# Leaky ReLU and residual sum of layer 1's input, moved from VectorE and GpSimd to ScalarE and TensorE, in a four-layer fused kernel

## The chip, the core and the metric

The kernel runs on one core of one Trainium2 chip. The core has four compute engines that run side by side, each with its own queue: TensorE (PE, matrix products), VectorE (DVE), ScalarE (ACT) and GpSimd (POOL). A fifth, SyncE (SP), only starts DMA transfers here. The metric is the device time of one launch, in microseconds; lower is better.

## The reference

The input is x, 16 images of 192 channels and 32 x 32 pixels (1024 pixels), in float32. Four layers follow, each of the form x = x + f(norm(x)). Layer 0 is an mLSTM block, then a 3x3 convolution, a batch norm over all images and a leaky ReLU. Layer 1 is channel attention, layer 2 a state-space block with a selective scan in four directions, layer 3 a convolution over weighted shifts. What the change touches is the end of layer 0 and the beginning of layer 1:

```python
# end of layer 0: y is the convolution's output
y = (y - mu) / jnp.sqrt(var + 1e-05) * bn_g[None, :, None, None] + bn_b[None, :, None, None]
return jnp.where(y >= 0, y, 0.01 * y)
...
x = x + _L0_conv_ref(_gn(x), ...)
x = x + _L1_conv_ref(_gn(x), ...)
```

So per image: scale and shift each channel, take the larger of y and 0.01 y, add x, and go on to layer 1's group norm.

## The kernel before, in words

**Two parts.** `layer0` runs layer 0 for all images, up to the convolution's output before its batch norm, which goes to DRAM (`ydram`). The batch norm needs statistics over all images, so only then can `LayersB` begin, which does the rest. `setup` (L992) makes the batch norm's scale `bsc` and shift `bsh`, one column per group of 96 channels.

**The row of scans.** In `LayersB`, layer 2's selective scan is the backbone. It is cut into units: 128 lanes (32 channels x 4 states) by 1024 pixels, 192 units per image, 3072 in all. A unit needs: on ACT a decay (`decay`, L1987), on POOL an input (`inputs`, L1994), on DVE the scan itself (`scan`, L2002) and the product with C (`outputs`, L2011), on PE the sum over states (`sums`, L2044). In every eighth unit (`pooled`, L789: unit number 3 modulo 8) POOL makes the product instead (`weigh`, L2007). The tiles of this row turn over: two `h` in PSUM, three `xs` and three `hc` in SBUF, two each of `dl` and `du`, which are reloaded from DRAM for every four units (`fetch`, L1966).

**The pieces between.** All other work runs in the gaps of that row, as three streams of pieces: `front` makes the next units' inputs (`ahead`, L1876), `before` is `complete` (L1460: layer 2's end and layer 3 of the image before), `after` is `prepare` (L1236: the end of layer 0, layer 1 and the start of layer 2 of the image after). Each `yield` names the engine of the next piece. The order is written out while the program is built: `scans` (L1737) goes unit by unit, emits the unit's own instructions, and lets a stream go on where `fits` (L1824) says that by the planner's own clocks there is room. Those clocks add fixed prices per instruction (`Metered.RATES`, L797) and do not see the chip. Where PE would be left without work, `warm` (L2049) puts in matmuls of zeros.

**DMAs.** All loads and stores of this part are started by SP, in the order in which the program emits them. `post` (L913) notes a transfer; `flush` (L932) or `need` (L922) sends it when the planner's clock says that its source is ready, or that it is needed. An image's end matters here: `prepare` of the image after next begins near unit 184 and runs over into the next image, while `complete` of the image just scanned begins with the load of that image's scan output (`yh<-yd`, posted at L1480) and of x (`cx<-x1d`), a matmul with `on384` for the mean (L1488) and a subtraction on DVE (L1491).

**The stage that changes** (`prepare`, L1252 to L1268), per image:

- ACT scales and shifts both channel groups of `y` in place (two passes of 96 x 1024);
- for each of four halves ACT writes 0.01 y into a PSUM bank, and DVE takes the maximum of y and that bank into y;
- for each channel group POOL adds y to x (96 x 1024);
- x is stored for later (`x0d`), and `norm6` (L1132) takes its statistics on ACT.

`y` lives in the slot `pb`, which has room for three groups, `x` in the slot `pa`. `whole` and `view` give both as slices of fixed tiles. Most helpers record their instructions through `Metered`, so that these carry the line L817 in the profile; groups are told apart by the tiles' names.

Of the kernel before, what the change touches and what calls it, by code (L numbers as in the profile page):

```python
# [11 lines left out]
F32 = mybir.dt.float32  # L12
BF16 = mybir.dt.bfloat16
AF = mybir.ActivationFunctionType
ALU = mybir.AluOpType
# [5 lines left out]
L = H * W  # L21
HL = L // 2
P6 = 96
# [8 lines left out]
def half(hf):  # L32
    return slice(hf * HL, (hf + 1) * HL)


def matmuls(nc, out, pairs):
    n = len(pairs)
    for i, (l, r) in enumerate(pairs):
        nc.tensor.matmul(out, lhsT=l, rhs=r, start=(i == 0), stop=(i == n - 1))
# [821 lines left out]
class LayersB:  # L861
# [130 lines left out]
    def setup(self):  # L992

        tc, nc, cx, wp, I, NB = self.tc, self.nc, self.cx, self.wp, self.I, self.NB
        dp = self.dp
        self.dqd = dp.tile([6, 128, 9, 128], F32, name="dqd")
        self.dvd = dp.tile([2, 2, 128, 9, P6], F32, name="dvd")
        self.vd = dp.tile([P6, 2, L], F32, name="vd")
        self.x0d = dp.tile([P6, 2, L], F32, name="x0d")
        self.x2d = dp.tile([P6, 2, L], F32, name="x2d")  # L1000
        self.xdr = dp.tile([K, 2 * N, L], F32, name="xdr")
        self.dld = dp.tile([K, 3, 128, L], F32, name="dld")
        self.dud = dp.tile([K, 3, 128, L], F32, name="dud")
        self.yd = dp.tile([3, 128, L], F32, name="yd")
        self.zd = dp.tile([NB, 3, 128, L], F32, name="zd")
        self.x1d = dp.tile([NB, P6, 2, L], F32, name="x1d")


        bn_g, bn_b = self.vec("bn_g", P6), self.vec("bn_b", P6)
        self.bsc = wp.tile([P6, 2], F32, name="bsc")  # L1010
        self.bsh = wp.tile([P6, 2], F32, name="bsh")
        with tc.tile_pool(name="b_pre0", bufs=1) as pre:
            st = pre.tile([P6, 2, NB, 12], F32, name="st")
            for a in range(2):
                nc.scalar.dma_start(
                    st[:, a], self.sdram[:, a * P6 : (a + 1) * P6, :].rearrange("b p s -> p b s")
                )
            mv = pre.tile([P6, 2, 2], F32, name="mv")
            for a in range(2):
                nc.vector.bn_aggr(mv[:, a, :], st[:, a].rearrange("p b s -> p (b s)"))  # L1020
            sd = pre.tile([P6, 2], F32, name="sd")
            nc.scalar.activation(sd, mv[:, :, 1], AF.Sqrt, bias=cx.eps5[0:P6])
            nc.vector.reciprocal(sd, sd)
            nc.vector.tensor_mul(self.bsc, sd, bn_g)
            nc.vector.tensor_mul(sd, mv[:, :, 0], self.bsc)
            nc.vector.tensor_sub(self.bsh, bn_b, sd)


        self.blk6 = wp.tile([P6, P6], F32, name="blk6")
        nc.vector.tensor_scalar(self.blk6, cx.blk6, 1.0 / L, None, op0=ALU.mult)  # L1030
        self.offb = wp.tile([P6, P6], F32, name="offb")
        nc.sync.dma_start(self.offb, I["c_off48"])
        self.temp = wp.tile([P6, 2], F32, name="temp")
        for a in range(2):
            for j in range(2):
                nc.sync.dma_start(
                    self.temp[48 * j : 48 * j + 48, a : a + 1],
                    I["temperature"][2 * a + j : 2 * a + j + 1].unsqueeze(0).to_broadcast([48, 1]),
                )

        self.dw2b = self.vec("dw_b", 128)
        self.pads = [wp.tile([128, H + 2, W + 2], F32, name="pad%d" % i) for i in range(2)]
        for t in self.pads:
            nc.gpsimd.memset(t, 0.0)

        self.xx = wp.tile([128, 3, L], F32, name="xx")
        self.fixed, self.turned, self.views, self.whole = {}, {}, {}, {}
        for tag, n, bufs in (("pa", 2, 1), ("pb", 3, 1), ("p4", 1, 2), ("c4", 1, 3), ("cx", 2, 1)):
            self.fixed[tag] = [wp.tile([128, n * L], F32, name=tag + str(i)) for i in range(bufs)]
            for i, t in enumerate(self.fixed[tag]):  # L1050
                (nc.gpsimd if i % 2 else nc.vector).memset(t, 0.0)
        c4 = self.fixed["c4"]
        self.fixed["o4"] = c4[0:2]
        self.fixed["d3"] = [c4[2][:, 256 * i : 256 * i + 256] for i in range(4)]
        self.fins = []
        self.ms = [wp.tile([128, 2, C], F32, name="m%d" % i) for i in range(2)]
        for t in self.ms:
            nc.gpsimd.memset(t, 0.0)
# [177 lines left out]
    def prepare(self, b):  # L1236

        nc, cx, sm, I = self.be, self.cx, self.sm, self.I
        one = lambda i: bass.ds(i, 1)
        ch = lambda a: slice(a * P6, (a + 1) * P6)  # L1240
        yield "SP", 0
        y = self.slot("pb", [P6, 2, L], "y0")
        self.post(y, y, self.ydram[one(b)].rearrange("o (a p) l -> p (o a) l", p=P6))
        x = self.slot("pa", [P6, 2, L], "x0")
        self.post(x, x, I["x"][one(b)].rearrange("o (a p) l -> p (o a) l", p=P6))
        wv = self.weight(I["w_vT"].rearrange("(a p) o -> p a o", p=128), [128, 2, C])
# [3 lines left out]
        wq_ = [w_qk(0)]  # L1250
        yield "SP", 2
        for a in range(2):  # L1252
            yield "ACT", 0, y
            self.need(y)
            nc.scalar.activation(
                y[:, a, :], y[:, a, :], AF.Identity, scale=self.bsc[:, a : a + 1], bias=self.bsh[:, a : a + 1]
            )
        for a in range(2):
            for hf in range(2):
                yield "ACT", 0  # L1260
                p = self.mm()[0:P6, :]
                nc.scalar.activation(p, y[:, a, half(hf)], AF.Copy, scale=0.01)
                yield "DVE", 0
                nc.vector.tensor_max(y[:, a, half(hf)], y[:, a, half(hf)], p)
            yield "POOL", 0, x
            self.need(x)
            nc.gpsimd.tensor_add(x[:, a, :], x[:, a, :], y[:, a, :])
        self.post(x, self.x0d, x)  # L1268
        yield from self.norm6(x)

# [2 lines left out]
        for a in range(2):  # L1273
# [4 lines left out]
            v = self.p4([P6, L], "v")  # L1278
# [4 lines left out]
        for m in range(3):  # L1283
# [11 lines left out]
            for t0 in (0, 4):  # L1295
                yield "PE", 0
                p = self.mm()
# [85 lines left out]
        for m_, w_ in ((m1, w1), (m2, wpf)):  # L1383
            yield "PE", 0, w_
            self.need(w_)
            p = self.mm()[0:P6, 0 : 2 * C]
# [5 lines left out]
        for hf in range(2):  # L1392
            for a in range(2):
                yield "PE", 0, vs[hf]
                self.need(vs[hf])
                p = self.mm()[0:P6, :]
# [4 lines left out]
        x = self.slot("pa", [P6, 2, L], "x1")  # L1401
# [6 lines left out]
        for a in range(2):  # L1408
            for hf in range(2):
                yield "PE", 0, x  # L1410
                self.need(x)
                p = self.mm()[0:P6, :]
# [30 lines left out]
        for gs in ((0, 1), (2,)):  # L1443
            zs = [self.p4([128, L], "z") for g in gs]
            for g, z in zip(gs, zs):
                for hf in range(2):
                    yield "PE", 0, wz
                    self.need(wz)
                    p = self.mm()
# [723 lines left out]
```

## Time and profile before

| | |
|---|---|
| median of 3 runs | 14432.32 us (14414.68 to 14432.79) |
| the profiled execution | 14423.57 us |
| its span, first to last instruction | 14421.8 us |
| mean granted TensorE clock | 0.924 |
| the row of scans | about 3320 to 14280 us |
| one image in it | 681 to 683 us |
| HBM traffic | 1338 MB read, 341 MB written |

A group line of the profile reads: line, engine, operation, output <- inputs by tile name (numbers left out), shapes, count | busy time in all, mean of one in ns | idle time of the engine just before them, and what ended it. A wait line reads: engine, the line that waited <- what it waited for: total us, times, longest. A line in order of time reads: start and duration in us, engine, line, what it does, and in brackets how long the engine had been idle and what released it. PE shows each float32 matmul as two rows. SP's instructions are the starts of transfers, whose data move after them.

### The profile page before, as it was taken

To read this page: it belongs to the slowest core of one execution; us is meant where nothing else is said; L and a number is where in the kernel's file an instruction comes from. 1 tells how busy PE (TensorE), PEld (TensorE's weight loads), DVE (VectorE), ACT (ScalarE), POOL (GpSimd) and SP (SyncE) were. 2 spreads that over 40 slices of the span, in tenths; PEclk is the share of its full clock that TensorE was granted. 3 is DMA by queue.
4 is the path that set the end of the run, shared out by engine and by line. 5 is a ranking of instruction groups with operands and counts; after the bars stand their busy time and mean duration, and the time that the engine had idled before them with its cause. 6 is when DMAs were issued, how large, how long until landed. Compare 5 with 4: busy or idle time off the path is not lost. (4 is left out here: it accounts for less than half of the span.)

```text
span 14421.8 us, 185702 instructions
## 1 busy us (share of the span) xinstructions
PE 12156.5 (84%) x68912; PEld 4993.1 (35%) x68912; DVE 11832.7 (82%) x9085; ACT 8688.4 (60%) x12229; POOL 10928.7 (76%) x6319
## 2 busy tenths in 40 slices
PE   8999999987888888888888888788888888888877
PEld 4444444442233333333333333333333333333323
DVE  4444444447899999999999999999999999999996
ACT  3333333336667676767676666676676767676655
POOL 2222222216799999999999999999999999999995
PEclk9999999998999999999999999998999999999888
DMA  1000000014344444444444445444444444444432
GB/s 29 15 16 16 15 16 16 16 40 131 128 157 143 157 154 159 153 143 158 143 158 141 160 145 164 142 159 137 162 134 164 147 157 162 145 152 150 144 122 90
DMA packets 702528, 1707.95 MB, mean 118 GB/s; under 512 B 125456, under 2 KB 260065, under 8 KB 693985
## 3 DMA queue, kind: packets, MB, share of 16 engines
q1 hardware_dynamic: 688928, 1693.28, 36.0%
q8 instruction: 556, 9.11, 0.3%
q10 hardware_dynamic: 12736, 3.04, 0.1%
q14 instruction: 308, 2.52, 0.1%
HBM read 1338.12 MB, written 341.15 MB: 116 GB/s over the span
## 5 line engine op out<-in xcount | busy, mean ns | idle before, releaser
L1994 POOL TENSOR_TENSOR xs<-du,bb 128x1024 f32<-128x1024 f32 x3072 | 7196.6, 2364 | 424.9 <-DVE h L2002 418.5
L2002 DVE TENSOR_TENSOR_SCAN h<-h,xs 128x1024 f32<-128x1024 f32 x2688 | 6150.8, 2288 | 385.5 <-ACT h L1987 296.1
L1987 ACT ACTIVATE h<-dl,A 128x1024 f32<-128x1024 f32 x3072 | 3413.9, 1113 | 2420.4 <-DVE hc L2011 2268.5
L2011 DVE TENSOR_TENSOR hc<-h,cb 128x1024 f32<-128x1024 f32 x2688 | 3290.6, 1224 | 264.9 <-DVE h L2002 4.6
L817 PE MATMUL mm<-pad,dg 128*128 128x512 f32 (+1 forms) x5580 | 2667.4, 616 | 120.3 <-DMA dg<-dvd 39.9
L2044 PE MATMUL acc<-hc,sel 128*32 128x256 f32 x24576 | 2016.5, 415 | 800.5 <-DVE hc L2011 600.5
L629 POOL TENSOR_TENSOR D<-D,mask 128x256 f32<-128x256 f32 x768 | 543.6, 741 | 2101.7 <-DVE D L626 2101.7
L2044 PEld LDWEIGHTS acc<-hc,sel 128*32 128x32 f32 x24576 | 549.6, 112 | 2745.4 <-DVE hc L2011 1397.2
L817 PEld LDWEIGHTS mm<-pad,dg 128*128 128x128 f32 (+1 forms) x5580 | 958.7, 182 | 1494.0 <-issue 1285.7
L2007 POOL TENSOR_TENSOR hc<-hc,cb 128x1024 f32<-128x1024 f32 x384 | 905.7, 2359 | 205.1 <-DVE hc L2002 201.9
L817 PE MATMUL mm<-pa,wgt 128*128 128x512 f32 (+1 forms) x1408 | 781.6, 681 | 208.0 <-ACT pb L817 119.6
L2052 PE MATMUL acc<-ones,zero 128*128 128x512 f32 x1648 | 901.6, 678 | 0.0
L2002 DVE TENSOR_TENSOR_SCAN hc<-h,xs 128x1024 f32<-128x1024 f32 x384 | 875.6, 2280 | 16.7 <-ACT h L1987 12.5
L817 POOL TENSOR_TENSOR dlh<-dlh,e 128x512 f32<-128x512 f32 x384 | 489.4, 1275 | 233.5 <-ACT e L817 230.9
L817 POOL TENSOR_TENSOR c<-cx 96x768 f32<-96x768 f32 (+4 forms) x510 | 650.2, 1298 | 2.5 <-PE mm L817 2.5
L817 PE MATMUL mm<-c,xT 128*96 128x256 f32 x2048 | 575.9, 423 | 69.0 <-ACT c L817 68.2
L2031 PE MATMUL acc<-y,ident 128*128 128x512 f32 x576 | 354.2, 700 | 250.1 <-ACT y L2063 248.8
L817 POOL TENSOR_TENSOR duh<-dlh,xx 128x512 f32<-128x512 f32 x384 | 538.1, 1401 | 30.1
L393 PE MATMUL pc<-ypad,w_c 128*64 128x512 f32 (+1 forms) x1152 | 480.3, 664 | 74.3 <-PEq L753 41.5
L2063 ACT COPY y<-acc 128x512 f32<-128x512 f32 x384 | 411.4, 1071 | 150.7 <-PE acc L2044 149.9
L626 DVE SCALAR_TENSOR_TENSOR D<-D,s 128x256 f32<-128x256 f32 x768 | 271.7, 416 | 255.6 <-ACT D L622 255.6
L2052 PEld LDWEIGHTS acc<-ones,zero 128*128 128x128 f32 x1648 | 329.4, 215 | 431.8 <-issue 429.5
(334 smaller groups left out, 15907.5 us busy)
## 6 DMA issues: line engine op xcount, KB each, us to landing
dl<-dld SPq DMA_DIRECT2D x768, 512.0 KB
du<-dud SPq DMA_DIRECT2D x768, 512.0 KB
bb<-xdr SPq DMA_DIRECT2D x256, 512.0 KB
cb<-xdr SPq DMA_DIRECT2D x256, 512.0 KB
dld<-dlh SPq DMA_DIRECT2D x384, 256.0 KB
dud<-duh SPq DMA_DIRECT2D x384, 256.0 KB
dg<-dqd SPq DMA_DIRECT2D x270, 192.0 KB
dg<-dvd SPq DMA_DIRECT2D x180, 144.0 KB
```

What stands on the lines that cost most here:

```text
L393: nc.tensor.matmul(p[r, :], lhsT=w_, rhs=v, start=(n == 0), stop=(n == 14))
L629: nc.gpsimd.tensor_mul(d, d, mask)
L817: return f(out, *args, **kw)
L1987: self.nc.scalar.activation(self.h[u % 2], self.dl[n % 2], AF.Exp, scale=self.A[:, blk, n : n + 1])
L1994: self.nc.gpsimd.tensor_mul(self.xs[u % 3], self.du[n % 2], self.bb[blk])
L2002: self.nc.vector.tensor_tensor_scan(o, h, x, 0.0, op0=ALU.mult, op1=ALU.add)
L2007: self.nc.gpsimd.tensor_mul(h, h, self.cb[u % BLOCKS])
L2011: self.nc.vector.tensor_mul(self.hc[u % 3], self.h[u % 2], self.cb[u % BLOCKS])
L2031: nc.tensor.matmul(acc, lhsT=self.cx.ident, rhs=self.y[:, g, half(pair)], start=True, stop=False)
L2044: nc.tensor.matmul(self.acc[rows4(q), q4(s)], lhsT=self.sel, rhs=part(q), start=False, stop=(s + blk == BLOCKS),)
L2052: self.nc.tensor.matmul(self.acc, lhsT=cx.zero.to_broadcast([128, 128]), rhs=cx.ones.unsqueeze(1).to_broadcast([128, 4, 128]), start=False ...
L2063: self.nc.scalar.copy(y.rearrange("p (s w h) -> p s h w" if k % 2 == 0 else "p (s h w) -> p s w h", s=2, **turn), self.acc.rearrange("p (s ...
```

## The change

The leaky ReLU is written as 0.99 relu(y) + 0.01 y. `setup` makes four small columns `leak`: scale and shift times 0.99 and times 0.01. Per channel group ACT now makes 0.01 y into a third group of `y`'s slot (Identity) and 0.99 relu(y) in place (Relu). For each half PE adds three products with the identity matrix in one PSUM bank (relu part, 0.01 part, x), and ACT copies the bank into x. DVE's maxima, ACT's copies into PSUM and POOL's additions are gone. The third group of the slot serves both channel groups, one after the other. The number of pieces in the stage stays at twelve.

```diff
+        self.leak = wp.tile([P6, 4, 2], F32, name="leak")
+        for i, share in enumerate((0.99, 0.01, 0.99, 0.01)):
+            nc.vector.tensor_scalar(self.leak[:, i, :], self.bsh if i // 2 else self.bsc, share, None, op0=ALU.mult)
...
-        y = self.slot("pb", [P6, 2, L], "y0")
-        self.post(y, y, self.ydram[one(b)].rearrange("o (a p) l -> p (o a) l", p=P6))
+        y = self.slot("pb", [P6, 3, L], "y0")
+        self.post(y, y[:, 0:2, :], self.ydram[one(b)].rearrange("o (a p) l -> p (o a) l", p=P6))
...
         for a in range(2):
-            yield "ACT", 0, y
-            self.need(y)
-            nc.scalar.activation(
-                y[:, a, :], y[:, a, :], AF.Identity, scale=self.bsc[:, a : a + 1], bias=self.bsh[:, a : a + 1]
-            )
-        for a in range(2):
+            for i, f in ((1, AF.Identity), (0, AF.Relu)):
+                yield "ACT", 0, y
+                self.need(y)
+                nc.scalar.activation(
+                    y[:, 2 * i + a * (1 - i), :], y[:, a, :], f,
+                    scale=self.leak[:, i, a : a + 1], bias=self.leak[:, 2 + i, a : a + 1],
+                )
             for hf in range(2):
+                yield "PE", 0, x
+                self.need(x)
+                p = self.mm()[0:P6, :]
+                matmuls(nc, p, [(cx.ident[0:P6, 0:P6], v[:, half(hf)]) for v in (y[:, a, :], y[:, 2, :], x[:, a, :])])
                 yield "ACT", 0
-                p = self.mm()[0:P6, :]
-                nc.scalar.activation(p, y[:, a, half(hf)], AF.Copy, scale=0.01)
-                yield "DVE", 0
-                nc.vector.tensor_max(y[:, a, half(hf)], y[:, a, half(hf)], p)
-            yield "POOL", 0, x
-            self.need(x)
-            nc.gpsimd.tensor_add(x[:, a, :], x[:, a, :], y[:, a, :])
+                nc.scalar.copy(x[:, a, half(hf)], p)
         self.post(x, self.x0d, x)
```

## The prediction

> **What bounds the kernel now.** I read the busy times first, then the groups by line, then the waits of VectorE (DVE) and of the DMA queue (SP), and last the order of time around one image's end. I call the i-th scan of an image "unit i" (0 to 191); 16 images make 3072 units. From the page:
>
> ```profile
> PE 12156.5 (84%) x68912; PEld 4993.1 (35%) x68912; DVE 11832.7 (82%) x9085; ACT 8688.4 (60%) x12229; POOL 10928.7 (76%) x6319
> L1994 POOL TENSOR_TENSOR xs<-du,bb 128x1024 f32<-128x1024 f32 x3072 | 7196.6, 2364 | 424.9 <-DVE h L2002 418.5
> L2002 DVE TENSOR_TENSOR_SCAN h<-h,xs 128x1024 f32<-128x1024 f32 x2688 | 6150.8, 2288 | 385.5 <-ACT h L1987 296.1
> L2011 DVE TENSOR_TENSOR hc<-h,cb 128x1024 f32<-128x1024 f32 x2688 | 3290.6, 1224 | 264.9 <-DVE h L2002 4.6
> ```
>
> From about 3320 to 14280 us the kernel is one long row of scans, in which DVE is 93 to 94% busy and POOL 92 to 95% (windows of 1000 us). A unit takes 3.53 us from scan to scan; every eighth, whose product POOL makes, 2.2 us. Images repeat every 681 to 683 us, so whatever delays a scan counts, times some 15 images. The longest single waits of that row are not ACT's. Next, lines from the waits of DVE and of SP:
>
> ```profile
> DVE h L2002 <- ACT h L1987: 296.1, 275, 12.3
> DVE yh L817 <- PE mm L817: 65.2, 15, 8.2
> SPq L1962 <- POOL xs L1994: 5653.1, 685, 15.9
> ```
>
> The second line is 4.3 us each: DVE stands before the first `yh` subtraction of `complete`, because the matmul before it waits for `yh`'s load. The third says that SP, one queue in order, spends 39% of the span holding a reload of `du` or `dl` until POOL has read the old one; all that stands behind it waits too.
>
> **The removed and added work.** Groups by line, and by tile name:
>
> ```profile
> L817 DVE TENSOR_TENSOR pb<-pb,mm 96x512 f32<-96x512 f32 x64 | 42.8, 672 | 4.7 <-ACT mm L817 4.6
> L817 ACT ACTIVATE mm<-pb 96x512 f32<-96x512 f32 x64 | 37.4, 586 | 24.2 <-DVE pb L817 24.2
> L817 POOL TENSOR_TENSOR pa<-pa,pb 96x1024 f32<-96x1024 f32 x32 | 75.4, 2357 | 22.4 <-DVE pb L817 22.4
> L817 ACT ACTIVATE pb<-pb,bsh,bsc 96x1024 f32<-96x1024 f32 x32 | 38.0, 1232 | 26.6 <-DMA pb<-ydram 20.8 <-DVE row L1104 5.8
> L817 ACT COPY pa<-mm 96x512 f32<-96x512 f32 x64 | 37.0, 578 | 17.9 <-PE mm L817 17.9
> L817 PE MATMUL mm<-pa,ident 128*96 128x512 f32 x128 | 69.0, 622 | 0.0
> ```
>
> DVE loses 64 maxima of 0.67 us. In the order of time one does not cost that much: with it a unit is 3.92 us long (scan starts 7450.03 and 7453.95), 0.39 over 3.53; behind a product, before a pooled scan, 1.74 between starts against 1.14 elsewhere, 0.60. Per image 3 x 0.39 + 0.60 = 1.77, and 15 images: **27 us saved**. Image 0 runs before the scans, where its DVE, POOL and ACT pieces overlap; I take 0, bounds -4 and +4.
>
> POOL loses 32 x 2.36 = 75 us. POOL waits for DVE 418 us and DVE for POOL's `xs` only 80 us in all, near units that hardly touch this stage; I take 0, bounds -10 and 0.
>
> ACT loses 64 x 0.586, gains 64 x 0.578 and 32 more full passes of 1.23: +39 us in 14400, with ACT 60% busy. It costs where a decay (L1987) comes late: summed unit by unit, ACT work beyond a unit's length is 52 us per image before and 53 after (row durations, order of both built programs), so 0, bounds -2 and +2 an image, -30 and +30. PE gains 192 f32 matmuls of 69.0/64 = 1.08 us, 207 us, less 9 fewer warming matmuls of 901.6/824 = 1.09, in 2265 us of idle: 0 of its own. Four tiny DVE scalings in setup: 4 x 0.1.
>
> Both kinds of ACT copy stand above: into PSUM 586 ns, out of PSUM 578 ns; so the new copies cost what the old did. The Trainium skill, "ScalarE: Activation LUTs", Step-by-step, says that ScalarE writes faster to PSUM than to SBUF, which speaks against turning these copies round; these rows do not show it. By the rule the 64 copies would cost more than before, by an amount that the page does not price; by the rows, 0.5 us less in all.
>
> **What the change moves.** The stage now goes ACT, PE, ACT one half after the other, with one third slot of `y` for both channel groups, and the planner, which fits pieces into units, ends it 5 units later: the last copy stands at unit 5 of the next image instead of the last addition near unit 0. Two things follow in the built order of images 3 to 14. The store `x0d<-pa` waits for that copy, and on SP it now comes after unit 5's `du` reload; behind it come `out_x`, the `out_proj` weights, and `yh<-yd`. Before, `yh` stood ahead of that reload. And the first `yh` subtraction stands in unit 7 instead of 6. Before, from the order of time around one image's end:
>
> ```profile
> 8152.16 2.28 DVE L2002 TENSOR_TENSOR_SCAN hc<-h,xs 128x1024 f32<-128x1024 f32 x1
> 8155.59 0.80 SPq L929 DMA_DIRECT2D yh<-yd  x1
> 8159.20 6.96 POOL L1994 TENSOR_TENSOR xs<-du,bb 128x1024 f32<-128x1024 f32 x3
> 8163.89 0.52 SPq L1962 DMA_DIRECT2D du<-dud  x1
> 8164.56 5.32 PE L817 MATMUL mm<-yh,on 128*128 128x512 f32 x6 [4.19 <-DMA yh<-yd]
> 8169.92 0.69 DVE L817 TENSOR_TENSOR yh<-yh,mm 128x512 f32<-128x512 f32 x1 [5.81 <-PE mm L817]
> ```
>
> Unit 3's scan ends at 8154.44; `yh` is issued 1.2 us later, PE starts 8.97 us after that, DVE 5.36 us after PE: the subtraction starts 15.5 us after unit 3's scan. The `du` reload goes when POOL's input for unit 7 ends (8163.87).
>
> After: behind unit 3's scan POOL makes unit 3's product (2.36), unit 6's input (2.36), now the two `res` additions (1.26 + 1.27), then unit 7's input (2.36): 9.6 us. SP then issues `du` (0.52), `x0d` (0.34), `out_x` (0.34), the weights (0.40): `yh` goes at 11.2 us, ten later than before. With 8.97 and 5.36 the subtraction starts at 25.5. One more unit (3.53) is done by then, so the loss is 25.5 - 15.5 - 3.53 = **6.5 us** an image. Bounds: the order of the units alone (one unit less between load and use) 3.5 us; with 1.3 MB of `du` and `x0d` just ahead of `yh`, at the 240 to 420 GB/s that windows of 4 us show there, 3 to 5 us more: 10.5. I take 6.5, since every term is a row. 12 images: 78 us. Image 1 (0.30 us wait before) gets its subtraction 1.5 units earlier for the same issue, image 2 (none) has `yh` behind the reload: about 5 each. Together **88 us lost**.
>
> Sum on the profiled execution, 14423.6 us (span 14421.8 + 1.8): -27 + 88 = +61, 14485. The median of the runs shown is 8.7 higher; there the forecast is **14493 us**.
>
> **Rivals.** (1) *Nothing measurable*: about +5, 14437, 22%. `yh` lands sooner than 8.97 us after its issue, or the ACT waits that follow (308 us over 15 images) shrink while DVE stands. For: image 11 waited 0.90 us where its neighbours wait 4 to 6. Against: ten images in twelve wait 3.7 us or more.
> (2) *Faster*: the maxima's 27 us come through, the long wait stays as long as before, and POOL's relief takes some of its 10: -35, 14397, 12%. Mechanism: the reload of `du` ahead of `x0d` and `yh` is released early because POOL, 4.7 us lighter per image, runs ahead. It decides from `yh` issued 4.7 us after unit 3's scan (1.2 + 3.53); against it stands unit 3's product on POOL, which alone needs 2.36 after that scan with 7.5 us behind it.
> (3) *Worse*: the bound of 10.5 us, 12 x 10.5 + 10 - 27 = +109, and ACT at +2 an image, +30: 14570, 14%.
> (4) PE becomes the bound through 207 us of matmuls: those in the way of the scans' sums would add up to 14 us an image; with 16% idle and warming matmuls to give way I put it inside (3).
>
> **How the numbers follow.** My forecast has 52%. The range takes in (1), the ACT bounds and most of (3): 14415 to 14560. What a measurement of this kernel tells from no change is 0.2%, 29 us: faster than 14403 is (2), 0.12; within, (1) and the lower edge of mine, 0.24; slower, 0.64.
>
> **What would show it.** Right: DVE's wait "yh <- PE mm" grows from 65 us to about 150; `yh<-yd` is issued after the `du` reload of unit 5, some 11 us after unit 3's scan; units 186 to 191 lose their 3.92 us steps; images repeat in 686 to 688 us. POOL busy falls by 75, ACT rises by 39, PE by 200. Wrong: `yh` issued within 5 us of unit 3's scan, or the sum of DVE's waits unchanged.

## The result, and the profile after

The changed kernel takes 14571.58 us (median of 5 runs, 14562.77 to 14597.44), the kernel before beside it 14430.91 (14414.68 to 14432.79): a ratio of 1.0105, 95% interval 1.0094 to 1.0115. By the medians it is slower by 140 us (the ratio would make it some 150); forecast were 61, and the range ended at 14560. The profiled execution took 14580.77 us (span 14579.0), 157 more than that of before.

From the page of the changed kernel: the busy times, and the groups that answer to those shown of before (busy us, mean ns of one | idle time ahead, and what ended most of it).

```profile
PE 12301.9 (84%) x69278; PEld 5008.8 (34%) x69278; DVE 11788.0 (81%) x9025; ACT 8717.6 (60%) x12257; POOL 10856.4 (74%) x6287
L1996 POOL TENSOR_TENSOR xs<-du,bb 128x1024 f32<-128x1024 f32 x3072 | 7194.1, 2364 | 550.2 <-DVE h L2004 545.0
L2004 DVE TENSOR_TENSOR_SCAN h<-h,xs 128x1024 f32<-128x1024 f32 x2688 | 6149.0, 2288 | 391.0 <-ACT h L1989 316.1
```

The busy times moved as forecast in sign and nearly in size: PE +145 (forecast 200), DVE -45 (43 for the maxima), ACT +29 (39), POOL -72 (75). DVE, which sets the pace, does 45 us less and ends 157 us later, so it stands about 200 us more. Where, the waits of DVE in the changed kernel tell (us in all, times, longest):

```profile
DVE h L2004 <- ACT h L1989: 316.1, 237, 11.5
DVE yh L817 <- PE mm L817: 181.2, 17, 14.9
DVE hc L2013 <- PE acc L2046: 33.4, 16, 2.7
DVE hc L2004 <- ACT h L1989: 32.1, 31, 2.9
DVE hc L2004 <- PE acc L2046: 23.7, 11, 2.7
```

The wait for `yh` grew by 116 us (65.2 before). The two waits for PE's sums (`PE acc`) were 2.2 and 0.5 us before and are 57 now: the prediction has no term for them. The two for ACT's decay grew by 40.

The stage's new rows are priced as the prediction put them: ACT's passes and the identity matmuls of `y`.

```profile
L817 ACT ACTIVATE pb<-pb,leak 96x1024 f32<-96x1024 f32 x64 | 79.3, 1239 | 19.4 <-DMA pb<-ydram 11.7 <-DVE row L1107 6.1 <-PE mm L817 1.2
L817 PE MATMUL mm<-pb,ident 96*96 96x512 f32 x256 | 133.2, 645 | 52.8 <-ACT pb L817 27.3 <-DMA xpj<-in_x_projT 23.2 <-ACT pa L817 2.3
```

The order of time around one image's end in the changed kernel, as shown of before (start, us):

```profile
8210.01 2.28 DVE L2004 TENSOR_TENSOR_SCAN hc<-h,xs 128x1024 f32<-128x1024 f32 x1
...
8221.83 0.51 SPq L1964 DMA_DIRECT2D du<-dud  x1
8222.44 0.54 SPq L929 DMA_DIRECT2D x0d<-pa  x1
...
8223.03 0.42 SPq L929 DMA_DIRECT2D out_x<-c  x1
...
8223.54 2.21 SPq L929 DMA_DIRECT2D wgt<-in_out_projT  x1
...
8225.85 2.59 SPq L929 DMA_DIRECT2D yh<-yd  x1
...
8236.02 5.46 PE L817 MATMUL mm<-yh,on 128*128 128x512 f32 x6 [14.05 <-DMA yh<-yd]
...
8241.52 0.69 DVE L817 TENSOR_TENSOR yh<-yh,mm 128x512 f32<-128x512 f32 x1 [14.85 <-PE mm L817]
```

This is the order that was forecast: `du` of unit 5, `x0d`, `out_x`, the weights, `yh`. Unit 3's scan ends at 8212.29; `yh` goes 13.6 us later (forecast 11.2), PE starts 10.2 us after that (8.97), DVE 5.5 after PE (5.36). The subtraction stands 29.2 us after unit 3's scan, not 25.5. As means of images 3 to 14, issue, landing and the way from PE to DVE are 13.6, 9.1 and 4.9 us here and 0.9, 8.6 and 4.8 before: 27.6 us in all against 14.2.

From the starts of all scans in the trace I worked out how long each stretch of units takes, as a mean of images 3 to 14 (us per image; the starts of units 0, 4, 6, 8, 44, 64, 184 and the next 0 subtracted). The kernels other than the first two are those of the experiments below.

| kernel | 0-3 | 4-5 | 6-7 | 8-43 | 44-63 | 64-183 | 184-191 | image |
|---|---|---|---|---|---|---|---|---|
| before | 13.57 | 7.49 | 12.63 | 125.49 | 70.53 | 423.64 | 29.23 | 682.58 |
| after | 12.76 | 8.64 | 21.42 | 125.55 | 74.70 | 421.05 | 29.83 | 693.94 |
| e1_order_only | 12.76 | 8.63 | 21.21 | 125.38 | 74.51 | 420.24 | 29.73 | 692.46 |
| h1_yh_first | 12.76 | 8.63 | 18.12 | 124.95 | 74.58 | 421.15 | 30.18 | 690.37 |
| f2_after_prefetch | 12.76 | 8.63 | 8.04 | 123.49 | 74.59 | 420.65 | 30.13 | 678.29 |
| f5_after_hoist | 12.76 | 8.63 | 8.04 | 124.16 | 69.90 | 420.87 | 30.00 | 674.36 |
| f3_before_pre_late | 13.53 | 7.46 | 8.04 | 123.39 | 73.34 | 422.05 | 29.51 | 677.33 |
| e4_before_max_small | 13.52 | 7.93 | 13.79 | 125.60 | 70.77 | 424.74 | 28.09 | 684.45 |
| f6_before_pre_max_small | 13.47 | 7.83 | 8.05 | 123.44 | 73.03 | 421.66 | 28.39 | 675.86 |

After against before: +11.4 us an image, of which units 6 and 7 (`yh`) give +8.8, units 44 to 63 +4.2, units 4 and 5 +1.2, and 64 to 183 -2.6. An image takes 693.9 us; forecast were 686 to 688. Units 44 to 63 lie some 150 us behind the stage that was changed. The order of time there, in the changed kernel:

```profile
8383.97 1.84 SPq L929 DMA_DIRECT2D dg<-dqd  x3
...
8392.25 4.28 PE L817 MATMUL mm<-pad,dg 128*128 128x512 f32 x6 [6.16 <-DMA dg<-dqd]
...
8398.12 2.29 DVE L2004 TENSOR_TENSOR_SCAN hc<-h,xs 128x1024 f32<-128x1024 f32 x1 [2.29 <-PE acc L2046]
```

`dg` are the taps of the second q/k convolution in `prepare`. In the built order before, their load goes in unit 41 of each image. The stage ends later now, all of `prepare` behind it moved with it, and the load goes in unit 47: behind the reloads of `bb` and `cb` on SP, which every direction needs in units 42 to 47. PE, in order, stands 6.16 us before it (its waits for `dg<-dqd` are 59.4 us in all, before 0.9), the sums queue up behind, and DVE finds no free `hc`. Theory 4 below comes from these lines.

### The profile page after: what moved, and what is told of

Read it like the earlier page. It is cut to its first block, busy times and chain, and to the rows that moved or that the text cites. A ratio compares the mean times of both kernels' runs of the same rounds, so it can differ in the third digit from the quotient of the medians.

```text
span 14579.0 us, 186332 instructions
## 1 busy us (share of the span) xinstructions
PE 12301.9 (84%) x69278; PEld 5008.8 (34%) x69278; DVE 11788.0 (81%) x9025; ACT 8717.6 (60%) x12257; POOL 10856.4 (74%) x6287
## 5 line engine op out<-in xcount | busy, mean ns | idle before, releaser
L2054 PE MATMUL acc<-ones,zero 128*128 128x512 f32 x1630 | 870.1, 664 | 0.0
L817 PE MATMUL mm<-xd,dtw 108*128 108x512 f32 x768 | 465.2, 690 | 14.3 <-ACT p L817 12.6
```

The lines of the kernel that those rows point to most:

```text
L817: return f(out, *args, **kw)
L2054: self.nc.tensor.matmul(self.acc, lhsT=cx.zero.to_broadcast([128, 128]), rhs=cx.ones.unsqueeze(1).to_broadcast([128, 4, 128]), start=False ...
```

## Theories

**Theory 1** (the prediction's): what is moved costs, by the late load of `yh`. **Theory 2**: the added matmuls on PE delay the scans' sums. **Theory 3**: the added ACT passes delay the decays. **Theory 4**: the waits for sums come from the load of `dg`, which the moved order puts behind other reloads; the added work has no part in it. Every kernel ran beside the kernel before, whose medians in the three groups were 14432.47 (first four), 14427.62 (next four) and 14424.17 us (last four). "Same order" means that the planner put every piece into the same unit; in e1, e2, e3 and f7 a few instructions of `setup` and image 0, ahead of the row of scans, stand in another order than in the kernel that they are compared with.

## Experiments on the changed kernel: work or order

**e1_order_only.** The planner is charged what the full work costs; the work itself is cut.

```diff
-                nc.scalar.activation(y[:, 2*i + a*(1-i), :], y[:, a, :], f, ...)
+                self.nc.scalar.activation(y[:, o, ::16], y[:, a, ::16], f, ...); self.charge("ACT", L)
-                matmuls(nc, p, [(ident, v[:, half(hf)]) for v in (...)])
+                matmuls(self.nc, p[:, 0:32], [(ident, v[:, half(hf)][:, ::16]) for v in (...)]); self.charge("PE", HL, 3)
-                nc.scalar.copy(x[:, a, half(hf)], p)
+                self.nc.scalar.copy(x[:, a, half(hf)][:, ::16], p[:, 0:32]); self.charge("ACT", HL)
```

> The changed kernel with its order kept to the last instruction, but with the work of the changed stage all but gone: the ACT passes, the identity matmuls and the copies out of PSUM of the stage take every sixteenth column only (so 15 of 16 columns of the batch norm, leaky ReLU and sum are left out); the planner is charged the full prices. Theory 1 (the moved order costs, through the late load of yh): the time stays near the changed kernel's 14572, at least 14520, and DVE's wait 'yh <- PE mm' stays at 160 to 190 us. Theory 2 (the matmuls added to PE delay the scans' sums) and theory 3 (the passes added to ACT delay the decays): the time falls to 14480 or below, DVE's waits on PE acc (57 us) or on ACT decay (348 us) fall by 40 us or more. If all of the loss is work: 14430.

Measured: 14548.87 us, ratio 1.0081 (1.0067 to 1.0094). With nearly all of the stage's work gone, all but 22 us of the loss stay. DVE still waits 177.0 us for `yh` and 54.6 for PE's sums; the table's row is that of the changed kernel to about 0.2 us in every stretch but one (64 to 183, -0.8).

**e2_pe_third** and **e3_act_third** take away PE's and ACT's part alone.

```diff
-   [(ident, v[:, half(hf)]) for v in (y[:, a, :], y[:, 2, :], x[:, a, :])]
+   [(ident, x[:, a, half(hf)])]; self.charge("PE", HL, 3)            # e2
-   activation(y[:, a, :], y[:, a, :], Relu, ...)
+   activation(y[:, a, 0:64], y[:, a, 0:64], Relu, ...); self.charge("ACT", L)   # e3
```

> The changed kernel, same order, with one of the three identity matmuls of each half (128 of 192 left out, 138 us of PE; the output lacks the leaky ReLU's term), planner charged for three. Theory 2: DVE's waits on PE acc fall from 57 us to about 20, the time by 30 us or more, to 14540 or below. Theory 1: the time stays within 15 us of 14572.

> The changed kernel, same order, with the two Identity passes of each image cut to 64 of 1024 columns (most of the 0.01 y term is left out; 32 passes of 1.23 us become 0.2, 33 us of ACT, about what the change added), planner charged in full. Theory 3: DVE's waits on the decay fall from 348 towards 309 us and the time by 25 to 40 us. Theory 1: within 15 us of 14572.

The edit of e3 cuts the Relu passes (`i == 0` in the code), not the Identity passes that its expectation names. Both are passes of 96 x 1024 with the same scale and bias columns, and there are 32 of each, so it still takes away the 33 us of ACT; what the output lacks is most of the relu term.

Measured: e2 14553.28 us, ratio 1.0088 (1.0074 to 1.0102), 18 us less than the changed kernel, a little over what theory 1 gave it; but DVE's waits for PE's sums stay at 55.8 us, so these do not come from the added matmuls, and theory 2 falls. One wait of `setup` and image 0, DVE's `p` for ACT's `pad`, went from 32.5 to 18.8 us, and the first scan starts 11.8 us earlier; whether less work on PE or the other order of `setup` shortened it was not tried. e3 14571.17 us, ratio 1.0096 (1.0080 to 1.0111): nothing that can be measured, though 33 us of ACT work are gone, and theory 3 falls as far as it speaks of work.

**f2_after_prefetch** moves one load.

```diff
             if t == 2:
                 self.scanned = b
+                if b > 0:
+                    self.pre = y = self.slot("cy", [128, 3, HL], "yh")
+                    self.need(self.y)
+                    self.post(y, y, self.yd[:, :, half(0)]...)
+                    self.posts[-1][0] = clock["DVE"]
...
+            elif hf == 0:
+                y = self.pre
```

> The changed kernel with one edit: the load of the first half of yh is posted at unit 2 of the next image, when the scan outputs are stored, instead of behind the tail of the image before it; in the built order it goes in unit 3, ahead of unit 5's reload of du and of the store of x0d, and the first subtraction stays in unit 7. Theory 1: the wait 'yh <- PE mm' falls from 181 us to below 40, and the time by 90 to 150 us, to 14420 to 14480. If DVE then meets other late work (decays, xs) behind the stage, less: 14500 to 14540. Theories 2 and 3: the time falls by 60 at most, since 94 us of the new waits are elsewhere.

Measured: 14390.55 us, ratio 0.9971 (0.9960 to 0.9983): 181 us less than the changed kernel, more than theory 1 gave it, and faster than before. The same image's end in f2:

```profile
8148.21 0.37 SPq L929 DMA_DIRECT2D yh<-yd  x1
...
8155.19 2.84 PE L817 MATMUL mm<-yh,on 128*128 128x512 f32 x6
...
8165.33 0.67 DVE L817 TENSOR_TENSOR yh<-yh,mm 128x512 f32<-128x512 f32 x1
```

and DVE's wait in all:

```profile
DVE yh L817 <- PE mm L817: 9.1, 2, 7.0
```

Hardly a wait is left, 9.1 of 181.2 us: the load goes ahead of the `du` reload, PE has its matmuls done 7 us before DVE comes to the subtraction. Nothing behind takes the gain back: units 6 and 7 fall from 21.42 to 8.04 us. The waits for PE's sums stay (54.9 us).

**h1_yh_first** asks which part of the lateness is SP's queue behind the reload.

```diff
     def flush(self):
-        for p in list(self.posts):
+        for p in sorted(self.posts, key=lambda p: p[1] is not getattr(self, "yh", None)):
```

> The changed kernel, same order of pieces; on SP the load of yh goes ahead of out_x and of the out_proj weights in unit 6, still behind the du reload of unit 5 and the store x0d. If the queue behind the reload makes the extra over the prediction (issue 13.6 us after unit 3's scan where 11.2 were put, landing 10.2 where 8.97): issue at about 10.8, landing about 9, the wait 'yh <- PE mm' falls from 181 us to 120 to 140, the time by 40 to 60, to 14510 to 14530. If the data ahead of it (du, x0d) set the landing: the wait falls by 20 at most, and the time to 14550 or above.

Measured: 14527.35 us, ratio 1.0072 (1.0058 to 1.0086), 44 us less; DVE's wait for `yh` 131.1 us.

```profile
8207.53 0.38 SPq L929 DMA_DIRECT2D yh<-yd  x1
...
8216.04 4.22 PE L817 MATMUL mm<-yh,on 128*128 128x512 f32 x6 [9.61 <-DMA yh<-yd]
...
8220.31 0.69 DVE L817 TENSOR_TENSOR yh<-yh,mm 128x512 f32<-128x512 f32 x1 [9.27 <-PE mm L817]
```

Unit 3's scan ends at 8196.67 here: issue after 10.9 us, landing 8.5, DVE 4.3 after PE. As means of images 3 to 14 issue and landing are 10.9 and 8.7 us, against 13.6 and 9.1 in the changed kernel. So the two issues ahead of `yh`, `out_x` and the weights, hold 2.7 us of its issue, where the prediction had put 0.74 us for both, and 0.4 of its landing; the rest of the wait stays, and belongs to the reload and to the unit in which `yh` is sent.

**f5_after_hoist** is f2 with the taps' load moved as well.

```diff
             yield from self.conv(qk, m % 2, 128, d)
+            if m < 2:
+                d = taps(m + 1)
             for t0 in (0, 4):
```

> The kernel f2_after_prefetch with one more edit: the taps (dg) of the next q/k convolution are posted right behind the convolution before it and not behind its transposes. The order of all pieces stays the same; only the load of dg goes in unit 45 instead of 47 of each image, ahead of the last reloads of bb and cb on SP (and in 58 instead of 61). Theory 4 (DVE's new waits for PE's sums, 55 us, come from PE standing some 5 us before that load near unit 48, where the moved order has put it): PE's wait on dg<-dqd falls from about 59 us to below 20, DVE's waits on PE acc from 55 to below 20, and the time by 30 to 55 us, to 14335 to 14360. If the sums are late because PE has too much work there: same time within 15 us of 14391.

Measured: 14337.62 us, ratio 0.9937 (0.9923 to 0.9950), 53 us less than f2 with all pieces in the same order. DVE's waits for PE's sums:

```profile
DVE hc L2023 <- PE acc L2056: 1.1, 2, 0.6
DVE hc L2014 <- PE acc L2056: 0.2, 1, 0.2
```

PE has no wait for `dg<-dqd` left (54.7 us in f2); the matmul that stood 6.16 us before `dg` waits 1.65 here, for ACT. Theory 4 is shown: 55 us of waits for PE's sums (54.9 in f2), and units 44 to 63 at 74.6 instead of 69.9 us, came from a load issued two units too late. PE had time for all its work there.

## Experiments on the kernel before: what the change is worth

**f3_before_pre_late**: the kernel before with f2's edit, and

```diff
-        self.sent[id(p[1])] = max(...) + LAND
+        self.sent[id(p[1])] = max(...) + LAND + (7.0 if p[1] is getattr(self, 'yh', None) else 0.0)
```

> The kernel before with the load of the first half of yh at unit 2, as in f2_after_prefetch, and with the planner's landing time for it 7 us longer, so that the first subtraction stands in unit 7. Its wait 'yh <- PE mm' should fall from 65 us to below 15. Theory 1 with nothing else: before gains 65 less what the waits behind it give back, 14370 to 14400, so that the change itself, with the late load mended on both sides, is worth between a loss of 20 and a gain of 20 us. If the change is a gain of its own (27 to 45 us for DVE's maxima): this kernel is 25 us or more slower than f2_after_prefetch, 14415 or above.

Measured: 14359.10 us, ratio 0.9951 (0.9938 to 0.9965), 68 us less than before: all 65 us of the wait come back (1.0 us is left). This is below the 14370 to 14400 that were expected. So moving the load of `yh` is worth 181 us in the changed kernel and 68 in the kernel before, a difference of 113; DVE's wait line grew by 116, and units 6 and 7 by 8.8 us an image, 105 over 12 images. f2 is 31 us slower than f3; f5, in which the second load is mended too, is 21 us faster.

But f3 is not free of late transfers. Its plan has moved too, and units 44 to 63 take 73.34 us in it instead of 70.53. From f3, behind the end of image 6:

```profile
8314.37 0.69 ACT L817 ACTIVATE dlh<-mm,v_dt_b 128x512 f32<-128x512 f32 x1 [5.16 <-DMA dld<-dlh]
...
8317.43 2.30 DVE L2011 TENSOR_TENSOR_SCAN h<-h,xs 128x1024 f32<-128x1024 f32 x1 [4.92 <-ACT h L1996]
```

In unit 52 ACT waits for the store `dld<-dlh`, which SP sends at 8307.77, behind the reloads of `du` and `dl`, and the decay behind it comes late: that unit takes 8.27 us on the mean, 3.5 before and in f5. (Before loses 1.5 us in unit 53 in the same way.) Between f3 and f5 these units make 3.44 us an image, 41 us over 12 images, twice the 21 by which f5 is faster; in all other units together f5 is 0.5 us an image slower. So whether the change is worth anything once no transfer is late stays open.

**e4_before_max_small** and **f6_before_pre_max_small** price the removed maxima, the one in the kernel before, the other in f3, where nothing waits for `yh`. **f7_before_pre_max_add_small** cuts the additions on POOL as well.

```diff
-                nc.vector.tensor_max(y[:, a, half(hf)], y[:, a, half(hf)], p)
+                self.nc.vector.tensor_max(y[..., ::16], y[..., ::16], p[:, ::16]); self.charge("DVE", HL)
-            nc.gpsimd.tensor_add(x[:, a, :], x[:, a, :], y[:, a, :])                        # f7
+            self.nc.gpsimd.tensor_add(x[:, a, ::16], x[:, a, ::16], y[:, a, ::16]); self.charge("POOL", L)
```

> The kernel before, same order, with DVE's 64 maxima taken over every sixteenth column (15 of 16 columns of the leaky ReLU left out; planner charged in full). The prediction's step (a maximum costs 0.39 us of a unit, 0.60 before a pooled one, 27 us in all): the time falls by 20 to 27 us, to 14404 to 14411. If each busy microsecond of DVE counts: 38 us, 14392. If DVE then only waits longer for ACT: within 8 us of 14430.

> f3_before_pre_late (the kernel before without the wait for yh) with the maxima over every sixteenth column, as in e4 (15 of 16 columns of the leaky ReLU left out), same order. In e4 the units 184 to 191 became 1.1 us shorter per image and the wait for yh 1.2 us longer. If that wait is what took the saving back: now 12 to 25 us faster than f3_before_pre_late (14359), 14334 to 14347. If another engine sets the pace of those units anyway: within 8 us of f3.

> As f6, and GpSimd's 32 additions also over every sixteenth column (the sum with x left out in 15 of 16 columns): 75 us of POOL become about 10. The prediction put them at 0 to 10 us. If POOL sets the pace there: 20 to 60 us faster than f6; if not, within 10 us of f6. Either way f5_after_hoist (14338) minus this is what the added work of ACT and PE and its order still cost.

Measured: e4 14430.34 us, ratio 1.0001 (0.9992 to 1.0010): nothing, where 20 to 27 us less were forecast. Units 184 to 191 do get 1.14 us shorter per image, and units 6 and 7 get 1.16 longer. SP sends `yh` 43.9 us after the start of unit 184 in both kernels (mean of images 3 to 14), so a DVE that is early only waits longer. The wait that took the saving back, in e4 (65.2 before):

```profile
DVE yh L817 <- PE mm L817: 81.2, 15, 8.1
```

f6: 14334.28 us, ratio 0.9943 (0.9929 to 0.9956), 25 us less than f3 by the medians, which are of two groups; 21 when each is taken against its own group's kernel before. Units 184 to 191 get 1.12 us shorter per image, 17 us over 15 images, and the saving is not taken back. So without the wait the maxima are worth some 17 to 25 us, where the prediction had 27. f7: 14336.65 us, ratio 0.9939 (0.9925 to 0.9952), 2 more than f6 by the medians: the additions on POOL cost nothing that can be measured.

## Two lighter forms

**g_one_pass** (on f5) and **g0_one_pass** (on the changed kernel, neither load moved) compute the same with two ACT passes fewer per image.

```diff
-   y = leak-scaled Identity(y) on ACT;  p = I y + I relu + I x;             x = copy(p)
+   (nothing on ACT)                     p = diag(0.01 bsc) y + I relu + I x;  x = Identity(p, bias=0.01 bsh)
```

> Computes the reference in full: f5_after_hoist with ACT's Identity pass left out. The 0.01 y term comes from a matmul of the raw y with a diagonal of 0.01 times the batch norm's scale, the shift is the bias of the copy out of PSUM; 32 ACT passes of 1.23 us (39 us) and their place in the plan go. From e3, where those passes were cut at no gain: within 15 us of f5_after_hoist. If a lighter plan also ends the stage earlier: 15 to 40 us faster, best of all kernels.

> Computes the reference in full: the changed kernel with ACT's Identity pass left out (0.01 y by a matmul of the raw y with a diagonal, the shift in the copy out of PSUM), and neither load moved. In its plan the stage ends earlier: yh is sent in unit 4 and first used in unit 6, as before the change, and the taps are sent in unit 44, not 47. Theory 1 with theory 4 (place of two loads in the plan): 14400 to 14460, though its work on ACT and PE is within 1% of the changed kernel's. If the work added to PE costs, or the form with PE as such: 14530 or above.

Measured: g_one_pass 14342.96 us, ratio 0.9941 (0.9928 to 0.9955), within noise of f5, as e3 had it for passes of the same length. g0_one_pass 14557.40 us, ratio 1.0095 (1.0079 to 1.0110): a miss by 100 us. In its plan `yh` and `dg` do stand nearly where they stood before, and units 44 to 63 are back (70.34 us), but `yh` is late all the same, now both halves of it (28 waits instead of 15):

```profile
DVE yh L817 <- PE mm L817: 164.2, 28, 9.4
```

Its units 0 to 3 take 16.88 us and units 8 to 43 131.66, both worse than in either kernel. So theories 1 and 4 tell what it costs when a load comes late, but the unit that the plan gives a load does not tell whether it will. By its expectation a time above 14530 speaks for the work on PE or for the form; against this stands g_one_pass, with the same stage and both loads moved, 214 us faster. In g0's units 0 to 3 DVE waits 1.9 us an image for POOL's `xs` and 2.0 for ACT's decays; what delays these, and the second half of `yh`, was not tried.

## Why the prediction was half right

The direction and the main mechanism were right; the size, 61 against 140 us, was not. By the runs the 140 are +113 (`yh`: 181 less 68), +53 (`dg`: f2 to f5) and -21 (f3 to f5: the change with both loads in time), together 145. These are differences along a chain of kernels, so the sum closes by construction, but for the 5 us by which the groups' kernels before differ; it is no check on the parts, and the -21 holds f3's late store. Step by step:

- **"The late `yh`": +88 forecast, 113 measured.** Mechanism, order on SP, and unit of the subtraction were as forecast. Issue: from the end of unit 7's input to the issue of `yh` the prediction put 1.6 us for `du`, `x0d`, `out_x` and the weights, from rows of before, where `x0d`, `out_x` and the weights did not stand directly behind a reload; behind one they took 4.0, the weights 2.21 of it instead of 0.40. The reference: the 15.5 us of before were those of image 7, the mean of images 3 to 14 is 14.2. Landing was 10.2 instead of 8.97 in image 7, but 9.1 on the mean. With the means an image loses 27.6 - 14.2 - 3.53 = 9.9 us; the prediction had 10.5 as its upper bound and took 6.5 "since every term is a row". The rows were of one image, and of another place in the queue.
- **The moved order was followed at one place only. This is the step that failed.** The text says "Two things follow in the built order". A third followed: all of `prepare` moves, and one of its loads, `dg`, meets the reloads of `bb` and `cb`. The prediction put that path at nothing; it measured 53 us (f2 to f5). Rival 4 put waits for sums at up to 14 us an image, but by PE's added work, which e1 and e2 exclude.
- **"27 us saved" by the maxima.** Right in size as a price for three of the four (units 188, 190 and 191 get 0.35 us shorter each in f6; 0.39 was put), wrong as a term: e4 shows that in the kernel before the saving is 0, since the wait for `yh` stands behind it and is ended by a load whose start does not move with DVE. A gain ahead of a wait that another engine or a DMA ends must not be added to the growth of that wait; in the sum above it stands inside the -21. The 0.60 us of the unit before the pooled one were hardly the maximum's: with the maximum cut in e4 that unit (186) goes from 4.77 to 4.67 us (means of images 3 to 14), while in the changed kernel, without it, the unit takes 3.92; what DVE waits for there was not followed.
- **POOL's additions 0**: right (f7). **ACT's work 0**: right as far as tried (e3, g_one_pass). But its moved pieces cost: the gelu of the image before now follows the pooled unit and holds unit 5's decay (units 4 and 5, +1.15 us an image), and in unit 184 ACT waits for the store `dld<-dlh` (3.68 us in image 7), by which that unit takes 5.73 us instead of 3.54. This eats what the maxima save there, and 184 to 191 end at +0.60 instead of -1.77. It is inside the -21. **PE's work 0**: nearly; e1 and e2 give 22 and 18 us at most.
- **The rows for the copies and passes** held: 1239 ns a pass (1232 before), 645 a matmul at the clock granted.

## What to carry to other kernels

When a hand-planned schedule shifts by a few units, follow every load that shifts with it through the in-order queue that starts it, for the whole period, not only next to the edit; the cost here came from the loads of `yh` and `dg` and hardly from the added work. Price the removal of work by the wait that ends next behind it: if another engine or a DMA ends that wait, the saving is zero until the wait is gone. And post a load when its source is ready rather than when its consumer's stage begins: that, with the first use one unit later, made the kernel before 0.5% faster (and one of its stores late, units 44 to 63), and with the taps' load turned the change from a loss into f5, 0.6% faster than before.

## What the chip showed beside that

**PE after standing.** The six matmuls on `yh` take 2.84 us in f2 and 5.46 in the changed kernel, where PE had stood 14 us. From the windows of the changed kernel, with the stretch in which PE waits and the one in which it runs them (window: length, busy us and instructions of PE, PEld, DVE, ACT, POOL; granted clock, DMA share, GB/s):

```profile
8222.00:8236.00 14.00, 0.00 (x0) 0.01 (x1) 4.56 (x3) 3.03 (x6) 9.19 (x5) 0.50 0.92 259
8236.00:8242.00 6.00, 5.98 (x14) 2.04 (x14) 0.48 (x1) 0.00 (x0) 0.00 (x0) 0.53 0.54 166
```

The granted clock is 0.50 while PE stands and 0.53 while it works through them; in f2, where PE had not stood, it is 1.00. So in this image the clock adds 2.6 us to the late load. Over images 3 to 14 the six take 4.2 to 5.5 us in the changed kernel, 4.9 on the mean, but 4.8 in the kernel before as well, where PE stood 2.0 to 4.2 us: late loads pay this in both kernels, and it is hardly part of the difference between them. The Trainium skill, "TensorE: Matmul & The Clock Gate", Part 1, states that TensorE falls to half its clock after an idle window of about 3.4 us and returns to full after as long a busy one; the fall agrees, with 0.50 in the 14 us in which PE stood; the return came later here, since 0.53 is the mean of 6 us with PE busy for 5.98.

**Issues in a row.** On SP the issue of `yh` takes 0.37 us in f2 and 0.38 in h1, where it is the third of the row that starts with a reload, and 2.59 us in the changed kernel, where it is the fifth, at 259 GB/s and a DMA share of 0.92. In h1 it is `out_x`, the fourth, that takes 2.82 us. The place in the row alone does not set it, since in f2 `x0d` takes 1.22 us as the second; what does was not tried.
